# PSUM copies of a token diffusion on VectorE, and a shifted norm two slots earlier in a local attention

## The chip, the cores and the metric

One core of one Trainium2 chip runs the whole program. The metric is the device time of one execution in microseconds (us); lower is better. All data are float32.

The engines of the core have a queue each and run side by side: TensorE (PE; its weight loads, PEld, are listed apart), VectorE (DVE), ScalarE (ACT), GpSimd (POOL) and SyncE (SP), which here issues DMAs. Matrix products land in PSUM, and another engine copies them from there to SBUF. A buffer of PSUM can be filled again only when its reader is done.

## What is computed

Four layers run one after the other on x, 8 sequences of 512 tokens of width 256. Each is `x = x + norm(layer(norm(x)))`: a differential attention, a local attention with a gated feed-forward (two layers deep), a token and channel diffusion, and a mixture of experts. The change touches the second and the third. Cut to what matters:

```python
# local attention and gated feed-forward, twice
h = shift_token(x)                       # half of the features come from the token before
q, k, v = split(h @ wqkv, 3)             # 8 heads of 64
q, k = rotary_xpos(l2norm(q) * qs, l2norm(k) * ksc)
x = x + local_attention(q, k, v) @ wo    # windows of 128, one window back
h = shift_token(x)
h = (h - h.mean()) / sqrt(h.var() + 1e-5) * lg + lb      # the "shifted norm"
a, g = split(h @ w1 + b1, 2)
x = x + (a * gelu(g)) @ w2 + b2

# token diffusion, 16 heads of 16
qk, v = x @ Wqk, x @ Wv
logits = (2 * qk @ qk.T - q2[:, None] - q2[None, :]) / sqrt(dh) * tau
out = softmax(logits) @ v @ Wo
# channel diffusion: the same over channels, 8 groups of 32 channels, on the next norm
```

## The kernel before

The program is written with a tile framework that assigns buffers, inserts the waits, and orders each engine's instructions by their place in the program, unless a priority says otherwise. `high_priority(offset=HOLD)`, with HOLD = 1000, moves an instruction ahead of up to that many others in its engine's order where its inputs allow. Stages are written as generators: work that fills the holes of other work yields, and a `Between` object takes the next part at each call.

**Copies.** `copy` (L156) brings a PSUM tile to SBUF. It takes ScalarE (L160) and VectorE (L162) in turn. `turned` transposes four blocks of 128 tokens into one PSUM bank and copies it; `project` makes a product of two token blocks and hands it to a function that reads it. `moments` (L184 statistics, L186 aggregation, and a step for the reciprocal deviation `rs`) and `normed` (L194) together make a norm over the rows of a tile.

**The local stage** (about 1330 to 2660 us). There are 16 passes c, one for each of two layers and eight sequences. In a pass, eight slots u = 0 to 7 each make the scores of a pair of heads and half the tokens (`scores`: product L642, mask addition L645, maximum, exponential, normalisation on GpSimd), then transpose and copy the weights of the slot before (`turned`, tile lpT), and after every second slot multiply them with the values (`attend`, tile lpo, copied to loT). All PSUM tiles of this stage come from one ring of four tiles of two banks.

In the holes of these slots run two generators. `rotated(c + 1)`, called r, makes queries, keys and values of the next pass: for each of four token blocks a product lqk, a sum of squares, the rotation on VectorE (L607) and GpSimd (L608, L609), and later the transposes (L616) and copies into lqT and lkT. `gated(c - 1)`, called g, finishes the pass before: the output projection is added to y, its rows are shifted by one token into `hs` (DMAs L715 and L716, a copy on GpSimd L717), the shifted norm is made (L720), `hs` is transposed into ghT (L564, L569), and then come the products with w1 (tile lpa), the gate and the products with w2. The table `slots` says how many steps of r and g each slot takes, in order. Half of a slot's calls (rounded up) come before its `turned`, half behind it.

**The diffusion** (about 2676 to 3290 us, and its last sequence's tail to about 3393 us). `tokens` runs over 32 groups of four heads, four token blocks each: `scores` fills two PSUM tiles tsa (L1084) and ScalarE takes their exponentials (L1088); `sums` multiplies these with the values into tpo (L1097) and copies tpo to toc (L1103); `divide` transposes toc and divides. For each sequence `queries` and `squares` make tkT and tqT (L1024, L1025, tq2, L1039), `values` makes tv (L985), and `finish` does what follows a sequence: it transposes to toT, projects with Wo (product pp<-dwo,toT), adds to y, makes the next norm and the channel diffusion (tiles cqk, wc, wvc) and adds the result to x (L950). `finish` and the gate of the experts, with its tiles xf and xT, run as generators between the scores of the next sequence. The tiles pt, pp, tpo and so on come from a ring of two single banks of PSUM; tsa comes from another ring of three tiles of two banks. The last sequence's `finish` runs alone, in the tail.

The program holds two forms of `tokens`, for positive and for other values of tau; with the inputs drawn here, tau is positive and the first form (`known`) is executed.

Of the kernel before, what the change touches and what calls it, by code (L numbers as in the profile page):

```python
# [39 lines left out]
HOLD = 1000  # L40
# [62 lines left out]
class Between:  # L103


    def __init__(self):
        self.work = []
# [13 lines left out]
class Net:  # L121
    def __init__(self, tc, a, out):
        self.tc, self.nc, self.a, self.out = tc, tc.nc, a, out
        self.flip = 0
        self.logs = False


    def begin(self, ctx):
# [26 lines left out]

    def copy(self, out, in_):  # L156

        self.flip ^= 1
        if self.flip:
            self.nc.scalar.copy(out, in_)  # L160
        else:
            self.nc.vector.tensor_copy(out, in_)  # L162
# [374 lines left out]
    def local(self, nb, early, first):  # L537
# [3 lines left out]
        with ExitStack() as ctx:  # L541
# [4 lines left out]
            nc, tc = self.nc, self.tc  # L546
# [227 lines left out]
            first, second = Between(), Between()  # L774
            r, g = first, second
# [10 lines left out]
            r.add(rotated(0))  # L786
            r.end()

            slots = ((g, r), (g, r), (g,), (r, r, r), (r, r, g), (r, r, g), (g, r), (g, r))
            for c in range(total + 1):  # L790
                if c + 1 < total:
                    r.add(rotated(c + 1))
# [74 lines left out]
    def diffusion(self, nb, rest):  # L867

        nc, g = self.nc, self.dw
        later = lambda n, b, **k: rest.enter_context(self.tc.tile_pool(name=n, bufs=b, side="right", **k))
        wk, small, ps = later("t_wk", 1), later("t_small", 3), later("t_ps", 2, space=PSUM)
        tiles = lambda x: [x[:, t, :] for t in range(NT)]
        last = (self.hand[0], wk.tile([P, NT, TH, 16], F32, name="tol", tag="tol"))

        def finish(b, y, o):

            yield
            yield  # L880
            oT = wk.tile([P, DC, S], F32, name="toT", tag="chT")
            self.turned(ps, o.rearrange("p t h e -> p t (h e)"), oT)
            yield

            def add(t0, pp):
                nc.vector.tensor_add(y[:, t0:t0 + 2, :], y[:, t0:t0 + 2, :], pp)

            for t0 in range(0, NT, 2):
                self.project(ps, lambda t: [oT[:, c, self.tok(t)] for c in range(DC)], [g["o"][:, c, :] for c in range(DC)], add, [t0])
                yield  # L890

            made = self.moments(small, tiles(y))
            yield
            h = wk.tile([P, NT, D], F32, name="th", tag="th")
            self.normed(tiles(y), tiles(h), *made)
            yield
            hT = wk.tile([P, DC, S], F32, name="chT", tag="chT")
            self.turned(ps, h, hT, g["g2"], g["b2"])
            yield
            qk = wk.tile([P, NT, D], F32, name="cqk", tag="cqk", bufs=1)  # L900
            for t0 in range(0, NT, 2):
                self.project(ps, lambda t: [hT[:, c, self.tok(t)] for c in range(DC)], [g["cqk"][:, c, :] for c in range(DC)],
                             lambda t0, pp: self.copy(qk[:, t0:t0 + 2, :], pp), [t0])
                yield
            pd = ps.tile([P, DC, P], F32, name="cpd", tag="ps")
            for i in range(DC):
                self.mm(pd[:, i, :], [(qk[:, t, self.tok(i)], qk[:, t, self.tok(i)]) for t in range(NT)])
            dot = small.tile([P, DC, P], F32, name="dot", tag="dot", bufs=1)
            nc.vector.tensor_copy(dot, pd)
            dg = small.tile([P, DC, P], F32, name="dg", tag="dg", bufs=1)  # L910
            nc.vector.tensor_mul(dg, dot, self.ident.unsqueeze(1).to_broadcast([P, DC, P]))
            yield
            pr = ps.tile([P, DC, P], F32, name="cpr", tag="ps")
            self.mm(pr, [(self.const[:, C_ONE:C_ONE + P], dg)])

            nc.vector.scalar_tensor_tensor(dot, dot, 2.0, pr, ALU.mult, ALU.subtract)
            for i in range(DC):
                nc.vector.scalar_tensor_tensor(dot[:, i, :], dot[:, i, :], g["ct"][:, i:i + 1],
                                               self.const[:, C_BLK:C_BLK + P], ALU.mult, ALU.add)
            nm = small.tile([P, DC], F32, name="cnm", tag="cnm")  # L920
            nc.vector.tensor_reduce(nm, dot, AX.X, ALU.max, negate=True)
            rs = small.tile([P, DC], F32, name="crs", tag="crs")
            for i in range(DC):
                nc.scalar.activation(dot[:, i, :], dot[:, i, :], AF.Exp, bias=nm[:, i:i + 1], accum_out=rs[:, i:i + 1])
            nc.vector.reciprocal(rs, rs)
            nc.vector.tensor_mul(dot, dot, rs.unsqueeze(2).to_broadcast([P, DC, P]))
            yield
            yield

            pw = ps.tile([P, DC, D], F32, name="cpw", tag="ps")  # L930
            for i in range(DC):
                self.mm(pw[:, i, :], [(dot[:, i, :], g["co"][:, i, :])])
            wc = wk.tile([P, DC, D], F32, name="wc", tag="wc", bufs=1)
            self.copy(wc, pw)
            yield
            pv = ps.tile([P, DC, D], F32, name="cpv", tag="ps")
            for i in range(DC):
                self.mm(pv[:, i, :], [(g["cv"][:, c, self.tok(i)], wc[:, c, :]) for c in range(DC)])
            wv = wk.tile([P, DC, D], F32, name="wvc", tag="wc", bufs=1)
            self.copy(wv, pv)  # L940
            yield
            yield
            for t0 in range(0, NT, 2):
                if t0:
                    yield
                self.project(ps, lambda t: [hT[:, c, self.tok(t)] for c in range(DC)], [wv[:, c, :] for c in range(DC)], add, [t0])
            made = self.moments(small, tiles(y))
            yield
            self.normed(tiles(y), tiles(y), *made)
            nc.gpsimd.tensor_add(self.xb(b), self.xb(b), y)  # L950
            yield
            self.between.add(self.gate(b, wk, small, ps))

        self.logs = True
        flag = nc.values_load(self.flag, min_val=0, max_val=1)
        with self.tc.If(flag > 0) as known:
            self.tokens(nb, True, wk, small, ps, finish, last)
        with known.Else():
            self.tokens(nb, False, wk, small, ps, finish, last)
        self.joint()  # L960
        self.between = Between()
        self.between.add(finish(nb - 1, *last))
# [5 lines left out]
    def tokens(self, nb, known, wk, small, ps, finish, last):  # L968
# [5 lines left out]
        with ExitStack() as ctx:  # L974
            pool = lambda n, b, **k: ctx.enter_context(self.tc.tile_pool(name=n, bufs=b, **k))
            step, big = pool("t_step", 2), pool("t_big", 3, space=PSUM)
            nc, g = self.nc, self.dw
            state, qk, es, pos, outs = {}, {}, {}, {}, {}
# [3 lines left out]
            def values(b, first=range(0, NT, 2)):  # L982
                hT = state[b][1]
                self.project(ps, lambda t: [hT[:, c, self.tok(t)] for c in range(DC)], [g["v"][:, c, :] for c in range(DC)],
                             lambda t0, pp: nc.scalar.copy(self.tv[b % 2][:, t0:t0 + 2, :, 0:16],  # L985
                                                           pp.rearrange("p t (h e) -> p t h e", e=16)), first)

            def prepare(b):
                y = last[0] if b == nb - 1 else wk.tile([P, NT, D], F32, name="ty", tag="ty", bufs=3)
# [51 lines left out]
            def heads(n):  # L1041

                b, r = divmod(n, 4)
                h = 8 * (r // 2) + r % 2
                return b, slice(h, h + 7, 2)
# [44 lines left out]
            def sums(n, k):  # L1090
                b, h = heads(n)
                if k == 0:
                    pos[n] = ps.tile([P, S], F32, name="tpo", tag="ps")
                e = es.pop((n, k))
                for i in range(4):
                    with self.tc.high_priority(offset=HOLD if i and known else 0):
                        m = nc.tensor.matmul(pos[n][group(i), :], lhsT=self.tv[b % 2][:, k, h.start + 2 * i, :], rhs=e[:, i, :],  # L1097
                                             start=k == 0, stop=k == NT - 1)
                        if i and known:
                            self.tc.keep_in_program_order(m)  # L1100
                if k == NT - 1:
                    oc = step.tile([P, S], F32, name="toc", tag="toc")
                    nc.scalar.copy(oc, pos.pop(n))  # L1103
                    outs[n] = oc

            def divide(n):
# [22 lines left out]
            for s in range(4 * (total + 1) if known else 0):  # L1129
                n, k = divmod(s, 4)  # L1130
# [17 lines left out]
                if k == 1 and n % 4 == 0 and n < total:  # L1148
                    if n // 4 + 1 < nb:
                        ahead.add(prepare(n // 4 + 1))  # L1150
                    if n:
                        b = n // 4 - 1
# [6 lines left out]
            for s in range(0 if known else 8 * (total + 2)):  # L1159
                n, j = divmod(s, 8)  # L1160
# [10 lines left out]
                if j == 5 and 0 <= n - 2 < total:  # L1171
                    divide(n - 2)
                    b = (n - 2) // 4
# [181 lines left out]
    def experts(self, nb, rest):  # L1355


        self.between.end()
        self.logs = False
        rest.close()  # L1360
        with ExitStack() as ctx:
            tiles = ctx.enter_context(ExitStack())
# [3 lines left out]
            nc, tc, g = self.nc, self.tc, self.ew  # L1366
# [191 lines left out]
```

## Time and profile before

| What | us |
|---|---|
| three runs: lowest, median, highest | 3804.09, 3808.49, 3828.85 |
| the profiled execution | 3837.43 |
| its span, from the first instruction to the last | 3835.7 |

The mean TensorE clock that was granted in it is 0.953 of full speed. Times in the profile are counted from the start of the span. In a row of the timeline stand the start, the duration, the engine, the line of the kernel, the operation, its tiles (out<-in), and in brackets the engine's idle time before it and what ended it.

Rows of single groups, that the change moves (mean ns of one, then idle time before it):

```
L985 ACT COPY tv<-pp 128x512 f32<-128x512 f32 x16 | 9.3, 578 | 4.5 <-PE pp L213 4.5
L1103 ACT COPY toc<-tpo 128x512 f32<-128x512 f32 x32 | 18.5, 580 | 14.8 <-issue 9.0 <-PE tpo L1097 5.8
L194 DVE TENSOR_SCALAR hs<-hs,mv,rs 128x256 f32<-128x256 f32 x64 | 37.9, 652 | 1.2 <-ACT rs L170 1.2
```

### The profile page before, as it was taken

The numbers are of one execution on the slowest core, as the hardware profiler recorded it, in microseconds if no ns is written. First come the engines' busy times: TensorE is split into PE (matmuls) and PEld (weight loads), VectorE is DVE, ScalarE is ACT, GpSimd is POOL, SyncE is SP. The second block draws the span as 40 slices with busy tenths as digits, with TensorE's granted clock in tenths as the row PEclk, the third lists the DMA queues.
The fourth block names the chain that finished last, engine by engine and source line by source line (L and its number), as shares of the span: only waits on it lengthen the run. The fifth ranks groups of instructions, "written<-read, shape, count | busy, mean of one in ns | idle before, by whom it ended". The sixth has DMA issues, their size and how long they took to land. (4 is left out here: it accounts for less than half of the span.)

```text
span 3835.7 us, 53567 instructions
## 1 busy us (share of the span) xinstructions
PE 3484.9 (91%) x20034; PEld 1894.1 (49%) x20034; DVE 2201.1 (57%) x4364; ACT 1855.1 (48%) x3719; POOL 1583.6 (41%) x1432
## 2 busy tenths in 40 slices
PE   8999999999987999999999999997988889679985
PEld 3344444444434566665665555564444444446554
DVE  6777777677646666665555666663244443344445
ACT  3555555555543444444444444443655555223334
POOL 3666766676654433333333343321012211153334
PEclk8999999999979999999999999998999999789997
DMA  9300000000001000000010000000000000421115
GB/s 350 119 1 7 6 7 1 7 7 1 6 6 34 3 4 4 4 4 25 4 34 9 9 9 9 9 20 23 1 23 23 23 17 17 147 68 55 53 43 167
DMA packets 95138, 130.29 MB, mean 34 GB/s; under 512 B 24702, under 2 KB 73242, under 8 KB 94874
## 3 DMA queue, kind: packets, MB, share of 16 engines
q1 hardware_dynamic: 88346, 108.94, 8.8%
q0 software_dynamic: 6528, 17.87, 1.3%
q8 instruction: 162, 2.65, 0.3%
q14 instruction: 102, 0.84, 0.1%
HBM read 57.40 MB, written 65.18 MB: 32 GB/s over the span
## 5 line engine op out<-in xcount | busy, mean ns | idle before, releaser
L372 ACT ACTIVATE e<-sa 128x1024 f32<-128x1024 f32 (+3 forms) x512 | 359.4, 702 | 303.7 <-PE sa L365 299.3
L393 POOL TENSOR_TENSOR e<-e,e 128x1536 f32<-128x1536 f32 (+2 forms) x192 | 451.7, 2353 | 91.4 <-PE po L388 81.4
L365 PE MATMUL sa<-qT,kT 32*128 32x512 f32 (+3 forms) x2048 | 431.9, 498 | 9.2 <-ACT e L372 8.8
L369 DVE TENSOR_REDUCE spread<-sc 128x2 f32<-128x256 f32 (+3 forms) x512 | 422.2, 825 | 15.3
L355 PE MATMUL sc<-kT,qT 32*128 32x128 f32 (+3 forms) x2048 | 421.6, 493 | 7.9 <-DVE spread L369 4.5
L656 ACT ACTIVATE lp<-lp,lnm 128x256 f32<-128x256 f32 (+1 forms) x512 | 240.1, 470 | 260.4 <-DVE lnm L648 156.0
L660 POOL TENSOR_TENSOR lp<-lp,lrs 128x1024 f32<-128x1024 f32 x64 | 121.1, 1893 | 529.0 <-DVE lrs L657 508.9
L368 DVE TENSOR_TENSOR sc<-sc,const 128x256 f32<-128x256 f32 x512 | 218.6, 427 | 173.7 <-PE sa L365 140.7
L1088 ACT ACTIVATE te<-tsa 128x1024 f32<-128x1024 f32 x256 | 248.9, 1023 | 135.8 <-PE tsa L1084 88.7
L355 PEld LDWEIGHTS sc<-kT,qT 32*128 32x128 f32 x2048 | 160.7, 189 | 284.9 <-DVE spread L369 113.1
L213 PE MATMUL lpa<-ghT,lw 128*128 128x512 f32 x640 | 284.8, 600 | 12.1 <-ACT ghT L569 12.1
L213 PE MATMUL lqk<-qkv,lhT 128*128 128x512 f32 x512 | 247.7, 622 | 2.3 <-DVE qk L607 1.6
L608 POOL TENSOR_TENSOR qk<-qk,over 128x1024 f32<-128x1024 f32 x64 | 151.4, 2366 | 207.8 <-DVE qk L607 207.8
L375 POOL TENSOR_SCALAR_AFFINE_SELECT e<-e 128x512 f32<-128x512 f32 x256 | 160.5, 640 | 177.0 <-ACT e L372 176.6
L1407 ACT ACTIVATE ehT<-eht,enorm 128x128 f32<-128x128 f32 x288 | 108.3, 457 | 208.6 <-PE eht L1403 207.7
L213 PEld LDWEIGHTS lpa<-ghT,lw 128*128 128x128 f32 x640 | 119.3, 190 | 163.3 <-issue 136.3
L388 PE MATMUL po<-e,v 128*32 128x512 f32 (+3 forms) x2048 | 188.3, 451 | 4.0 <-POOL e L375 3.6
L365 PEld LDWEIGHTS sa<-qT,kT 32*128 32x128 f32 x2048 | 160.9, 190 | 56.4 <-ACT e L372 29.7
L645 DVE TENSOR_TENSOR lp<-lsc,const 128x768 f32<-128x768 f32 (+1 forms) x128 | 138.6, 1083 | 86.5 <-PE lsc L642 85.9
L642 PE MATMUL lsc<-lkT,lqT 64*128 64x256 f32 (+1 forms) x1024 | 156.9, 386 | 28.1 <-DVE qk L607 28.0
L1084 PE MATMUL tsa<-tqT,tkT 32*128 32x512 f32 x1024 | 170.2, 673 | 5.9 <-DVE tqT L1039 3.3
L213 PE MATMUL py<-ew,ehT 128*128 x576 | 145.3, 397 | 23.5 <-ACT ehT L1407 23.5
(294 smaller groups left out, 6811.7 us busy)
## 6 DMA issues: line engine op xcount, KB each, us to landing
xrows<-zero SPq DMA_DIRECT2D x66, 514.0 KB
ex<-xrows SPq DMA_DIRECT2D x72, 128.5 KB
ew<-in_L_ffn_w_dram SPq DMA_DIRECT2D x16, 512.0 KB
egot<-yrows SPq DMA_DIRECT2D x16, 512.0 KB
x<-in_L_attn_X_dram SPq DMA_DIRECT2D x8, 512.0 KB
saved<-x SPq DMA_DIRECT2D x8, 512.0 KB
lx<-saved SPq DMA_DIRECT2D x8, 512.0 KB
xf<-xf SPq DMA_DIRECT2D x8, 512.0 KB
```

What stands on the lines that cost most here:

```text
L213: self.nc.tensor.matmul(out, lhsT=l, rhs=r, start=i == 0, stop=i == len(pairs) - 1)
L355: nc.tensor.matmul(sc[:, i, :w], lhsT=qT[g, self.tok(t)], rhs=kT[g, :w], start=True, stop=True)
L365: nc.tensor.matmul(sa[:, i, :S - k * P], lhsT=kT[g, self.tok(k)], rhs=qT[g, k * P:], start=True, stop=True)
L368: nc.vector.tensor_add(sc[:, :, w - P:w], sc[:, :, w - P:w], own)
L369: nc.vector.tensor_reduce(self.spread[n % 2][:, t, g0:g0 + 2, 0 if n % 2 else 16], sc[:, :, :w], AX.X, ALU.max, negate=True)
L372: nc.scalar.activation(x[:, h0:h0 + 2, :], sa[:, :, :S - k * P], AF.Exp, scale=0.25)
L375: nc.gpsimd.affine_select(x[:, :, :P], x[:, :, :P], [[0, 4], [1, P]], ALU.is_ge, 0.0, base=0, channel_multiplier=-1)
L388: nc.tensor.matmul(pos[n][group(g), k * P:], lhsT=seqs[b][1][:, k, 4 * r + g, :], rhs=x[:, g, :], start=k == 0, stop=k == 2)
L393: nc.gpsimd.tensor_add(y, y, es.pop((n, k)))
L656: nc.scalar.activation(x, x, AF.Exp, bias=nm[:, i, k:k + 1], accum_out=rs[:, i, k:k + 1])
L1084: m = nc.tensor.matmul(sa[i // 2][:, i % 2, :], lhsT=kT[q, self.tok(k)], rhs=qT[q, :], start=True, stop=True)
L1088: nc.scalar.activation(e[:, 2 * i:2 * i + 2, :], sa[i], AF.Exp)
```

## The change

Three edits:

1. A switch `held` is on from the start of the diffusion until the experts. While it is on, every `copy` is one on VectorE with high priority, and the turn between the two engines is not taken.
2. The copies of tv and toc, so far always on ScalarE, go through `copy`. The two additions of products to y in `finish` get the high priority.
3. In the local stage, slots 3, 4 and 5 change from `(r, r, r), (r, r, g), (r, r, g)` to `(r, g, r, r), (r, r), (r, r, g)`. The shifted norm, the second step of g, is so written in slot 3, after the first step of r and before the weights' `turned`, instead of in slot 4 at its end. The number of steps of each generator stays; as half of a slot's calls are made before `turned`, some steps of r also change sides.

```diff
@@ -155,6 +156,11 @@
     def copy(self, out, in_):
 
+        if self.held:
+
+            with self.tc.high_priority(offset=HOLD):
+                self.nc.vector.tensor_copy(out, in_)
+            return
         self.flip ^= 1
         if self.flip:
             self.nc.scalar.copy(out, in_)
@@ -786,7 +792,7 @@
-            slots = ((g, r), (g, r), (g,), (r, r, r), (r, r, g), (r, r, g), (g, r), (g, r))
+            slots = ((g, r), (g, r), (g,), (r, g, r, r), (r, r), (r, r, g), (g, r), (g, r))
@@ -883,7 +889,8 @@
             def add(t0, pp):
-                nc.vector.tensor_add(y[:, t0:t0 + 2, :], y[:, t0:t0 + 2, :], pp)
+                with self.tc.high_priority(offset=HOLD):
+                    nc.vector.tensor_add(y[:, t0:t0 + 2, :], y[:, t0:t0 + 2, :], pp)
@@ -952,6 +959,7 @@
         self.logs = True
+        self.held = True
         flag = nc.values_load(self.flag, min_val=0, max_val=1)
@@ -982,8 +990,8 @@
-                             lambda t0, pp: nc.scalar.copy(self.tv[b % 2][:, t0:t0 + 2, :, 0:16],
-                                                           pp.rearrange("p t (h e) -> p t h e", e=16)), first)
+                             lambda t0, pp: self.copy(self.tv[b % 2][:, t0:t0 + 2, :, 0:16],
+                                                      pp.rearrange("p t (h e) -> p t h e", e=16)), first)
@@ -1100,7 +1108,7 @@
-                    nc.scalar.copy(oc, pos.pop(n))
+                    self.copy(oc, pos.pop(n))
@@ -1357,6 +1365,7 @@
         self.logs = False
+        self.held = False
```

## What the change does to the time, predicted before it ran

> **What bounds the kernel now.** First the page, for the balance of the engines; then the busy time by windows, for the two stages that the change touches.
>
> ```profile
> PE 3484.9 (91%) x20034; PEld 1894.1 (49%) x20034; DVE 2201.1 (57%) x4364; ACT 1855.1 (48%) x3719; POOL 1583.6 (41%) x1432
> ...
> core 0: us, PE busy (x) PEld busy (x) DVE busy (x) ACT busy (x) POOL busy (x), PEclk, DMA share, GB/s
> 1330.00:2550.00 1220.00, 1175.73 (x6274) 737.05 (x6273) 747.49 (x1198) 566.35 (x1431) 436.99 (x316) 0.99 0.04 11
> 2676.00:3290.00 614.00, 549.19 (x3260) 271.32 (x3260) 246.78 (x764) 360.54 (x509) 98.46 (x111) 0.95 0.05 17
> 3290.00:3393.00 103.00, 52.88 (x186) 33.22 (x185) 33.30 (x111) 10.61 (x24) 39.53 (x55) 0.68 0.50 154
> ```
>
> The windows are the local stage, the diffusion loop and the last sequence's tail. TensorE is busy for 1175.73 of 1220 us, 549.19 of 614 and 52.88 of 103, so time can only come out of its idle 44 us, 65 us and 50 us. VectorE has room everywhere (40% busy in the loop), ScalarE too. A copy is therefore worth what TensorE waits for it, not its own duration. So I read the timeline for TensorE's waits. Local stage, one (layer, sequence) pass of 90.8 us (columns: start, duration, engine, line, operation; in brackets the idle time before it and what ended it):
>
> ```profile
> 1841.26 2.35 POOL L608 TENSOR_TENSOR qk<-qk,over 128x1024 f32<-128x1024 f32 x1 [2.39 <-DVE qk L607]
> 1843.69 1.90 POOL L609 TENSOR_TENSOR qk<-qk,ss 128x1024 f32<-128x1024 f32 x1
> 1845.64 1.09 PE L616 MATMUL lpt<-const,qk 128*128 128x128 f32 x8 [0.71 <-POOL qk L609]
> 1850.26 1.13 PE L642 MATMUL lsc<-lkT,lqT 64*128 64x256 f32 x8 [1.85 <-DVE qk L607]
> 1853.15 2.56 DVE L194 TENSOR_SCALAR hs<-hs,mv,rs 128x256 f32<-128x256 f32 x4
> 1862.80 1.44 ACT L569 ACTIVATE ghT<-lpt,lb,lg 128x512 f32<-128x512 f32 x2
> 1863.62 10.57 PE L213 MATMUL lpa<-ghT,lw 128*128 128x512 f32 x24 [1.50 <-ACT ghT L569]
> ```
>
> The shifted norm (`hs`) runs at 1853.15; its transposes, ghT and then the gated product (lpa) come out of it, and lpa waits 1.50 us for ghT. Other waits here are for the rotated heads (POOL L609) and for a ring buffer that DVE L607 frees. Diffusion loop:
>
> ```profile
> 2896.11 0.58 ACT L160 COPY toT<-pt 128x512 f32<-128x512 f32 x1 [0.42 <-PE tsa L1084]
> 2896.19 0.69 DVE L162 COPY toT<-pt 128x512 f32<-128x512 f32 x1 [5.04 <-PE tsa L1084]
> 2896.74 3.57 PE L213 MATMUL pp<-dwo,toT 128*128 128x256 f32 x8 [1.26 <-ACT toT L160]
> ...
> 2946.79 2.37 POOL L950 TENSOR_TENSOR x<-x,ty 128x1024 f32<-128x1024 f32 x1 [1.19 <-DVE ty L194]
> 2949.19 1.41 DVE L184 BATCH_NORM_STATS2 st<-x 128x6 f32<-128x256 f32 x4 [2.49 <-POOL x L950]
> 2951.35 0.57 ACT L985 COPY tv<-pp 128x512 f32<-128x512 f32 x1
> 2951.97 1.13 PE L213 MATMUL tq<-tsq,const 128*128 128x512 f32 x2 [2.30 <-ACT tv L985]
> 2956.40 0.66 PE L205 MATMUL pt<-const,xf 128*128 128x128 f32 x4 [0.96 <-DVE tqT L1039]
> ```
>
> One toT copy starts late on ScalarE (its queue is full of exponentials), and the product behind it waits 1.26 us; tq waits 2.30 us for the ring buffer that tv's copy frees.
>
> **The change part by part.** The sum is made against the profiled execution, 3837.43 us (span 3835.7), which lies 0.76% above the median of the three runs, 3808.49; I carry the difference over to the median.
>
> *The copies.* In the branch that runs, 80 copies go from ScalarE to VectorE: tv 16 at 578 ns (row tv<-pp), toc 32 at 580 ns, and one each per sequence of toT, cqk, wc and xT, 32 at about 585. ScalarE loses 46.6 us, VectorE gains 80 x 0.69 (row DVE toT) = 55 us, about 302 of 614 us busy. That raises no bound; what counts is order. From the two kernels' instruction orders, per sequence:
> - toT: both halves now stand on VectorE directly behind their transposes, where it was idle for 5.04 us. The waits of pp<-dwo,toT sum to 10.1 us over the six full sequences; two VectorE copies end to end leave about 0.3 us of each. Gain 1.3 to 1.7; I take 1.5.
> - tv: its first copy now stands on VectorE behind four statistics of x, which wait for POOL's addition L950 (ends 2949.16), three more, and a normalise. VectorE executes in order, so it can't pass them. By their rows it ends near 2952.85 rather than at 2951.92: tq's wait grows from 2.30 to about 3.2. Loss 0.9.
> - toc: 0.11 us dearer, but no longer behind an exponential of 1.02 us, so it ends 0.6 earlier. The tqT chain, for which pt<-xf waits (0.96 us), comes behind tv and toc and ends at 2956.95 instead of 2956.34. That 0.6 and the dearer copy make a loss of 0.7 for tv and toc together.
> - cqk, wc, xT and the additions to y with high priority: their consumers stand at least one run of exponentials (4 us) behind in TensorE's order, and that run hides them. Without that cover each would cost at most its 0.11 us difference. If VectorE were late, they would cost its backlog, up to the 2.5 us wait above.
>
> Net −1.5 + 0.7 = −0.8 us x 6 = −5 us. In the tail TensorE and VectorE take turns, so a copy on the dearer engine counts in full: about 4 x 0.11 to 0.15 = +0.5 us. The moves add no DMA there.
>
> *The shifted norm, fourth slot instead of the end of the fifth.* Per pass, the 4 statistics, 4 aggregations, ScalarE's two steps for rs, 4 normalisations and later 8 transposes and ghT all stay; only place changes. The four DMAs that shift the rows are issued 1828.88 to 1831.26 and land about 3 us later; the statistics now stand at 1836.8, so near 2.5 us of slack is left, and SP's queue has nothing behind them that is needed sooner. Replaying the slots by hand with the rows above: three statistics ahead of the sums of squares delay the heads' chain by 0.29 us (L609 ends 1845.87 for 1845.59). rs is ready at 1842.75. Then the four normalisations. Alone they cost 4 x 0.40 = 1.6 us, but here they meet two POOL operations back to back. The profile has that neighbour too:
>
> ```profile
> 1318.47 2.76 DVE L194 TENSOR_SCALAR x<-x,mv,rs 128x256 f32<-128x256 f32 x2
> 1318.63 2.45 POOL L608 TENSOR_TENSOR qk<-qk,over 128x1024 f32<-128x1024 f32 x1 [0.56 <-DVE qk L607]
> 1321.16 1.90 POOL L609 TENSOR_TENSOR qk<-qk,ss 128x1024 f32<-128x1024 f32 x1
> 1322.02 1.19 DVE L194 TENSOR_SCALAR x<-x,mv,rs 128x256 f32<-128x256 f32 x1
> ```
>
> A normalisation that starts beside L608 ends with it, and a later one ends with L609. **A rule speaks against the change here.** The Trainium skill, page "SBUF — State Buffer", on the port pair that VectorE and GpSimd share, calls it an exclusive lock: whoever starts first holds it for the whole instruction, and the other is fully blocked. hs where it runs now meets one lock (2.56 us for 1.6). By the rule the new place can meet two, so the norm ends at about 1846.7, as in the rows above; by hs's own row it ends at 1845.3, and unblocked at 1844.4. What waits behind it on VectorE is the mask addition (L645) of the next scores, its maximum, and the copy lpT, which attention needs. With the double lock lpT is ready at 1849.8, the last heads end at 1855.6, and the gated product starts at 1862.8 instead of 1863.62: −0.8 us a pass. With one lock −1.8, with none −2.1. I take −0.8, the nearest row for the neighbour. 14 steady passes: −11 us. The bounds are −29 us, and, if VectorE runs later than I replay, a loss (below).
>
> Sum: −11 − 5 + 0.5 = −16 us: the profiled execution 3821, the median 3792.
>
> **The rivals.**
> *Faster (0.16).* The normalisation misses the locks (−2 x 14 = −28), and the diffusion's ring waits shrink as the edit says, tv included because the statistics' wait on L950 also shortens: six times the waits for toT 1.5, tv 1.5, tqT 0.7 = −22. About −50: 3758. For: 65 us of idle TensorE in that window. Against: tv's place in VectorE's order.
>
> *Hidden (0.14).* Nothing in the local stage moves, because lpa's start is set by the attention chain (lpo, loT) and not by ghT. Only diffusion's −5 to +5 is left: 3803 to 3813. For: ghT's wait is only 1.50 us, and half of it can return as the next wait.
>
> *Slower (0.20).* VectorE's order in the fourth slot. Normalisations held by both locks stand in front of the mask addition L645, which frees the lsc buffer and feeds the exponentials. In the replay the break-even is an end of the norm near 1847.5, only 0.8 us behind the one that I take. Past it every us goes through lpT, lpo, loT and the last heads. If the norm instead makes POOL wait (the lock works both ways), L609 ends late and the transposes at 1845.64, which wait for it already, slip in full. At 1.5 us lost a pass, +21; with tv's 0.9 x 6 = +5, about +26: 3835. With both, up to 3 us a pass, it passes 3850. For: waits at 1845.64 and 1850.26 show that the heads' chain is critical in just these slots. Against: VectorE is only 61% busy.
>
> That the change doesn't do what it says is out: the order shows all 80 copies and the moved norm.
>
> **How the numbers follow.** The forecast, −5 to −35 us, has 0.50; its own range is 3774 to 3804. The range leaves out the far halves of the faster and the slower case: 3764 to 3835. One per cent, 38 us (below 3770 or above 3847), is about what a measurement can tell from no change. Faster by that takes most of the faster case: 0.13. Slower takes the part of the slow case with 3 us a pass: 0.10. Within it: 0.77.
>
> **What would show it.** In the changed profile the pass's period falls from 90.8 to about 90.0; hs's normalisations last about 3.9 us where they overlap L608 and L609; lpa's wait for ghT shrinks and lqk's heads end later than lpa's other inputs. tq's wait is led by VectorE's tv and is near 3.2 us; the waits for toT are below 0.5 us. I am wrong if the period grows, if the transposes' wait at L616 grows, or if TensorE's idle time in the loop stays near 65 us with new names.

## The result, and the profile after

The changed kernel takes 3823.51 us (median of 13 runs, 3812.63 to 3828.62), the kernel before 3810.6 us (13 runs, 3804.09 to 3828.85): a ratio of 1.0028, 95% interval 1.0015 to 1.0041. It is slower by 0.28%, about 11 us, where 16 us less was forecast. Yet the profiled execution of the changed kernel has a span of 3811.9 us, 24 less than the 3835.7 of the profile that the prediction was made from. So the first thing to settle is which two profiles can be compared.

The changed kernel's page has this line of busy times:

```profile
PE 3478.5 (91%) x20034; PEld 1898.6 (50%) x20034; DVE 2287.4 (60%) x4444; ACT 1811.1 (48%) x3639; POOL 1582.8 (42%) x1432
```

The 80 copies have moved: ScalarE is 44 us down and VectorE 86 us up, about 52 of it behind the local stage and 31 in it, where the moved norms last longer. TensorE's work is the same 20034 instructions. Busy time by window, cut where the stages begin: the local stage from the first projected sum, the diffusion loop from its first tsa to its last, then tail and experts. The changed kernel:

```profile
core 0: us, PE busy (x) PEld busy (x) DVE busy (x) ACT busy (x) POOL busy (x), PEclk, DMA share, GB/s
1277.20:2658.30 1381.10, 1318.12 (x6955) 825.48 (x6953) 867.78 (x1383) 631.31 (x1583) 482.81 (x359) 0.98 0.04 12
2658.30:3259.90 601.60, 550.40 (x3254) 271.67 (x3256) 293.22 (x829) 318.34 (x433) 97.06 (x109) 0.94 0.05 17
3259.90:3811.90 552.00, 416.56 (x1660) 280.91 (x1652) 259.29 (x699) 185.49 (x506) 207.30 (x287) 0.89 0.29 92
```

The kernel before, in the later profile before_again (span 3804.7 us), cut the same way:

```profile
1273.60:2666.80 1393.20, 1318.94 (x6959) 822.67 (x6957) 837.15 (x1383) 633.74 (x1584) 483.40 (x359) 0.98 0.04 12
2666.80:3255.60 588.80, 541.43 (x3256) 269.15 (x3256) 244.65 (x754) 357.23 (x507) 97.19 (x109) 0.95 0.05 18
3255.60:3804.70 549.10, 416.07 (x1660) 278.63 (x1652) 256.13 (x694) 188.44 (x511) 207.43 (x287) 0.89 0.29 92
```

The local stage is 12.1 us shorter, about as forecast. The loop is 12.8 us longer, and tail with experts 2.9 us longer. The last figure is not clear of scatter: the first stage, which the change does not touch, differs by 3.6 us. In the profile of the prediction the same loop of the same kernel had lasted 609.8 us: against that one the changed loop looks 8 us faster, against this one 13 slower. What decides here is therefore the ratio of runs on one chip, and profiles from one chip.

The local stage of the changed kernel, timeline of one pass (start, duration, engine, line, operation; idle time before it and what ended it):

```profile
1832.34 2.35 POOL L614 TENSOR_TENSOR qk<-qk,over 128x1024 f32<-128x1024 f32 x1 [2.57 <-DVE qk L613]
1833.48 3.98 DVE L200 TENSOR_SCALAR hs<-hs,mv,rs 128x256 f32<-128x256 f32 x4
1834.77 1.90 POOL L615 TENSOR_TENSOR qk<-qk,ss 128x1024 f32<-128x1024 f32 x1
...
1839.29 1.22 DVE L168 COPY lpT<-lpt 128x1024 f32<-128x1024 f32 x1
1840.56 1.09 PE L696 MATMUL lpo<-lpT,lv 128*64 128x128 f32 x16 [1.30 <-DVE lpT L168]
...
1853.14 5.42 PE L219 MATMUL lpa<-ghT,lw 128*128 128x512 f32 x12 [0.45 <-ACT ghT L575]
```

The shifted norm takes 3.98 us where it took 2.56: it is held by both POOL operations, one after the other (its first normalisation ends at 1834.84, 0.15 us behind L614's end). TensorE's wait for ghT is down from 1.50 to 0.45 us, and a wait of 1.30 us for the copy lpT, which stands behind the norm on VectorE, is new.

The diffusion loop of the changed kernel, the place where tq waits:

```profile
3011.23 2.37 POOL L957 TENSOR_TENSOR x<-x,ty 128x1024 f32<-128x1024 f32 x1 [1.19 <-DVE ty L200]
3013.63 1.40 DVE L190 BATCH_NORM_STATS2 st<-x 128x6 f32<-128x256 f32 x4 [2.48 <-POOL x L957]
...
3016.50 0.68 DVE L162 COPY tv<-pp 128x512 f32<-128x512 f32 x1
3017.24 1.13 PE L219 MATMUL tq<-tsq,const 128*128 128x512 f32 x2 [3.13 <-DVE tv L162]
```

From the start of the statistics to tq it is 3.61 us; in before_again it is 2.78 (3011.07 to 3013.85). TensorE waits 3.13 us before tq where it waited 2.29 there.

### The profile page after: what moved, and what is told of

Read it like the earlier page. It is cut to its first block, busy times and chain, and to the rows that moved or that the text cites. A ratio compares the mean times of both kernels' runs of the same rounds, so it can differ in the third digit from the quotient of the medians.

```text
span 3811.9 us, 53546 instructions
## 1 busy us (share of the span) xinstructions
PE 3478.5 (91%) x20034; PEld 1898.6 (50%) x20034; DVE 2287.4 (60%) x4444; ACT 1811.1 (48%) x3639; POOL 1582.8 (42%) x1432
## 5 line engine op out<-in xcount | busy, mean ns | idle before, releaser
L614 POOL TENSOR_TENSOR qk<-qk,over 128x1024 f32<-128x1024 f32 x64 | 151.0, 2360 | 173.2 <-DVE qk L613 171.4
L670 POOL TENSOR_TENSOR lp<-lp,lrs 128x256 f32<-128x256 f32 (+1 forms) x128 | 103.0, 825 | 220.2 <-DVE lrs L663 220.2
```

## The experiments

They ran on five chips, here called A to E. The medians of the kernel before were 3810.8, 3815.6, 3841.0, 3838.7 and 3840.2 us, so only ratios within a chip are compared. The ratios below are to the kernel before on the same chip, with their 95% intervals.

### Chip A: which of the two parts loses

Theory A: the moved norm gains and the copies lose more. Theory B: the moved norm loses in the runs that were not profiled.

slots_only, the kernel before with

```diff
-            slots = ((g, r), (g, r), (g,), (r, r, r), (r, r, g), (r, r, g), (g, r), (g, r))
+            slots = ((g, r), (g, r), (g,), (r, g, r, r), (r, r), (r, r, g), (g, r), (g, r))
```

> Only the slot table of the local stage is changed. Theory A (the moved norm shortens each pass from 90.8 to about 89.2 us as the profile of the changed kernel shows, and the loss comes from elsewhere): the local stage (first product behind the first pass to the first tsa) is about 12 us shorter and the whole about 3798 us, ratio 0.997. Theory B (the moved norm is the loss, in the runs that were not profiled): ratio at or above 1.003.

copies_only, the changed kernel with that line turned back:

> All edits of the diffusion, the old slot table. Theory A (the copies cost more than the moved norm gains, by waits on VectorE or by a lower TensorE clock in the diffusion loop): about 3810 + 13 + 12 = 3835 us, ratio near 1.006, and a granted clock below that of the kernel before. Theory B: ratio at or below 0.999.

Each kernel once more, for a second profile, after_again and before_again:

> The changed kernel once more, for a second profile. If the clock decides, an execution of about 3824 us shows a longer diffusion loop than the 601.6 us of the first profile (3813.6 us), with more time at half clock there, and a local stage that is unchanged (1381 us from the first projected sum to the first tsa).

> The kernel before once more, for a second profile and its granted clocks run by run. If the clock decides, its runs lie near 3810 us at a mean clock near 0.955, above the 0.949 that the changed kernel's runs show in the middle, and its diffusion loop lasts about 600 us in a usual run, less than the 609.8 of the profile of before (3837.4 us).

Measured: slots_only 3800.16 us, ratio 0.9968 (0.9955 to 0.9982); copies_only 3836.25 us, 1.0062 (1.0047 to 1.0078); after_again 3818.71 us, 1.0022 (1.0013 to 1.0031); before_again 3810.83 us, 1.0004 (0.9992 to 1.0016). Theory A holds, and the parts add up: 0.9968 x 1.0062 = 1.0030. The moved norm is worth 10.7 us, the copies cost 25 us. The second profile of the changed kernel repeats the first (loop 601.8 us), that of the kernel before doesn't (588.8 for 609.8). slots_only is faster than both kernels.

Where the local stage's gain comes from is read in the waits of TensorE (who waits for whom: us in total, times, longest). Before_again:

```profile
PE lsc L642 <- DVE qk L607: 24.0, 13, 1.9
PE lpa L213 <- ACT ghT L569: 12.1, 13, 1.5
PE lpt L616 <- POOL qk L609: 9.3, 13, 0.7
```

slots_only:

```profile
PE lpo L690 <- DVE lpT L162: 20.4, 15, 1.8
PE lpo L690 <- DVE lp L645: 7.4, 13, 0.6
PE lpa L213 <- ACT ghT L569: 4.1, 9, 0.5
PE lsc L642 <- ACT lv L624: 3.1, 7, 0.5
```

45.4 us of waits are down to 35.0 in these rows. The norm that left the later slot frees the ring buffer and the heads' chain there, and it delays lpT where it went.

### Chip B: is it tv's place on VectorE?

Theory T: tv's copy stands behind statistics that wait for POOL, and this wait, made longer, is the loss. Rivals: the loss is spread over the other copies; or what matters is not the wait but TensorE's clock.

tv_on_act, copies_only with tv back:

```diff
-                             lambda t0, pp: self.copy(self.tv[b % 2][:, t0:t0 + 2, :, 0:16],
+                             lambda t0, pp: nc.scalar.copy(self.tv[b % 2][:, t0:t0 + 2, :, 0:16],
```

> The edits of the diffusion with the old slot table, but tv's copies stay on ScalarE. Theory T (tv's place on VectorE behind the statistics of x makes the wait, and the longer wait trips the half clock): the wait of tq falls back from 3.2 to 2.3 us a sequence, the time at half clock in the loop from 87 to about 57 us, and the time from 3836 to about 3811 us, ratio 1.000. Rival S (the loss is spread over toc, toT, cqk and the additions to y on a fuller VectorE): ratio stays above 1.004.

tv_alone, the kernel before with nothing but tv's copy on VectorE with high priority:

> The kernel before with only the copies of tv moved to VectorE with high priority. Theory T: most of the loss, ratio about 1.005, tq waits 3.2 us, half clock near 80 us in the loop. Rival S: ratio below 1.002.

fill, copies_only with added products ahead of tq (cut; `self.zero` is a tile of zeros):

```diff
+                for j in range(5 if known and k == NT - 1 and n % 4 == 2 else 0):
+                    for i in range(4):
+                        with self.tc.high_priority(offset=HOLD):
+                            m = nc.tensor.matmul(pos[n][group(i), :], lhsT=self.zero, rhs=e[:, i, :], start=False, stop=False)
```

> The edits of the diffusion with the old slot table, and in the gap ahead of the waiting tq 20 more matmuls a sequence (zeros times the exponentials, added to tpo, so the result is the same; about 2.4 us of TensorE work that lies inside the 3.2 us wait). Theory C (the half clock that the gap brings is the larger part of the loss, not the gap): the half clock around tq goes, 20 to 40 us of it in the loop, and the time falls by 8 to 20 us, from 3836 to 3816 to 3828, though TensorE does more work. Rival W (only the wait itself counts): 3836 or slower, by up to 14 us if the added work isn't hidden.

tvf3_slots, the changed kernel with the gate's statistics behind tv (cut; `self.head` is tv's last copy):

```diff
+        yield
+        yield
+        yield
+        with ExitStack() as order:
+            if self.head is not None:
+                order.enter_context(tc.issue_after(self.head))
+            made = self.moments(small, tiles(self.xb(b)))
-        made = self.moments(small, tiles(self.xb(b)))
```

> The whole change, and the statistics of x for the experts' gate are put behind tv's copy in the order (three steps later in the generator, and ordered behind the copy), so that no copy stands on VectorE behind the wait for GpSimd. Theory T: tq's wait falls to under 1 us a sequence, time at half clock in the loop to 40 us or less, the loop to about 575 us and the time to about 3785 us, ratio 0.993. Rival (the later gate is waited for in turn by xT, the gate's product or the ring behind it): ratio 0.997 or above, the gain of the slot table alone.

Measured: tv_on_act 1.0043 (1.0028 to 1.0058), tv_alone 1.0005 (0.9996 to 1.0014), fill 1.0116 (1.0094 to 1.0137), tvf3_slots 1.0147 (1.0127 to 1.0166). Theory T falls on this chip by tv_alone: tq waits 18.8 us in all instead of 13.8, the loop still lasts 589.0 us (588.8 in before_again on chip A), and the time is the same. A wait of TensorE that grows isn't yet time lost.

tv_on_act says less than it seems to. With tv back on ScalarE tq was expected to wait 2.3 us again; it still waits 3.14. Before_again, then tv_on_act:

```profile
3009.63 1.92 PE L1097 MATMUL tpo<-te,tv 128*32 128x512 f32 x16
3013.85 2.08 PE L213 MATMUL tq<-tsq,const 128*128 128x512 f32 x2 [2.29 <-ACT tv L985]
...
3023.74 1.13 PE L219 MATMUL tq<-tsq,const 128*128 128x512 f32 x2 [3.14 <-ACT tv L993]
3024.80 1.07 PE L1105 MATMUL tpo<-te,tv 128*32 128x512 f32 x8
```

tv's copy is as early as before, 2.77 us from the statistics to tq. But 8 of the 16 tpo products now stand behind tq, so TensorE comes to tq earlier and waits longer for it. Moving toc with high priority makes this: toc_alone has the same order of TensorE's instructions as tv_on_act, while pairs_alone and no_priority (below) have that of the kernel before. Nor is the half clock around tq the loss here: in tv_on_act the loop has 56.3 us at half clock, as before_again has 56.7, and 0.43% is still lost.

fill decides nothing on the clock, since it didn't do what it was meant to. Its timeline:

```profile
2965.54 4.47 PE L1108 MATMUL tpo<-te,zero 128*32 128x512 f32 x40
...
2975.57 0.95 PE L213 MATMUL pt<-const,xf 128*128 128x128 f32 x4 [2.43 <-DVE toc L164]
```

The added products took 4.47 us, not 2.4; they delayed toc, and the gap came back one step later, with the half clock behind it (89.5 us of it in the loop, 87.1 in that of copies_only).

In tvf3_slots the waits of TensorE are these:

```profile
PE tpt L1129 <- DVE toc L162: 11.4, 4, 4.2
PE pt L211 <- DVE th L200: 6.8, 4, 1.9
PE pt L211 <- DVE toc L162: 5.7, 2, 5.4
PE tsa L1099 <- ACT te L1103: 5.6, 9, 2.7
```

tq's wait is gone from the list, and waits for toc and the exponentials have taken its place; the loop is 627 us. The gate also ends later, which lengthens the tail: tail and experts take 575.9 us.

### Chip C: the other copies, and the priority

pairs_alone keeps only the switch in `copy` (toT, cqk, wc, wvc, xT), on the kernel before (cut):

```diff
+        if self.held:
+
+            with self.tc.high_priority(offset=HOLD):
+                self.nc.vector.tensor_copy(out, in_)
+            return
```

> The kernel before with only the copies of toT, cqk, wc, wvc and xT held on VectorE with high priority; tv and toc stay on ScalarE, the additions to y as before. Theory D (two halves that two engines copied side by side now stand one behind the other on VectorE, 0.7 us a pair, which counts in full where TensorE and VectorE take turns): the tail up to the experts' first transposes about 2.8 us longer (110.4 for 107.6), the loop 4 to 10 us longer, ratio 1.002 to 1.004. Rival E (the loss belongs to toc, whose 32 copies reorder TensorE's products): ratio at or below 1.001.

toc_alone changes only toc (`moved` is a copy on VectorE with high priority, as above; tv_alone uses it for tv):

```diff
-                    nc.scalar.copy(oc, pos.pop(n))
+                    self.moved(oc, pos.pop(n))
```

> The kernel before with only the 32 copies of toc on VectorE with high priority. Theory D: ratio near 1.000 to 1.001, the tail unchanged at about 107.6 us. Rival E: ratio 1.003 or more, by a longer loop.

no_priority is copies_only without any high priority, the additions' too (cut to the copies):

```diff
         if self.held:
 
-            with self.tc.high_priority(offset=HOLD):
-                self.nc.vector.tensor_copy(out, in_)
+            self.nc.vector.tensor_copy(out, in_)
             return
```

> All copies and additions of the diffusion's edits on VectorE, but none with high priority; old slot table. Theory D (the engine, not the priority): about as slow as with priority, ratio 1.005 to 1.007. Rival P (the priority puts short copies ahead of the normalisations on the chain and reorders the products): ratio below 1.003.

Measured: pairs_alone 1.0020 (1.0006 to 1.0033), toc_alone 1.0025 (1.0013 to 1.0036), no_priority 1.0050 (1.0031 to 1.0070). The loss is spread: pairs and toc together give 1.0045, and tv_on_act, which holds both, gave 1.0043 on chip B. Rival P falls: without priority, and with TensorE's order as before, the copies are about as slow as with it. The high priority of the two additions was not run by itself.

### Chips D and E: added waits, or the half clock

The records of TensorE's clock know two states, full and half, and change in steps of 3.41 us. Theory H: the moved copies cost by the time at half clock, not by added waits; then TensorE's busy time grows by half of the added time at half clock. Rival W: added waits.

Chip D had the kernel before and the three parts alone, chip E the kernel before, copies_only and tv_on_act; the edits are those above.

> The kernel before, for a profile on the same chip as the three parts of this call. Its loop and its time at half clock there are what the parts are compared with; by theory H (a part costs by the half clock that its shifted waits bring) the loop's busy time on TensorE differs between the kernels by half of the difference in time at half clock, within 2 us.

> Only toc's copies on VectorE, once more, beside a profile of before on the same chip. Theory H: loop 8 to 12 us longer than before_c's, most of it busy time of TensorE with 10 us or more of added half clock. Rival W (added waits alone): TensorE's idle time in the loop up by 6 us or more and its busy time within 3 us.

> Only the copies of toT, cqk, wc, wvc and xT on VectorE, once more. Theory D (halves one behind the other): tail about 1 to 3 us longer than before_c's; and the loop 4 to 8 us longer. Theory H or rival W for the loop, as for toc.

> Only tv's copies on VectorE, once more: the way from the statistics of x to tq is 0.84 us longer than in before_c as in the first profile of the whole change, the loop within 3 us of before_c's, ratio 1.000 to 1.001.

> The kernel before, for a profile on the chip of this call: the loop near 589 us if this chip is of the first kind (as in the first four experiments), near 620 us if it is of the second.

> All edits of the diffusion, old slot table, on another chip. Theory H: the loop's TensorE busy time grows over before_d's by half of what the time at half clock grows by, within 3 us (14.4 us for 30.5 us in the first pair), and the waits add about 4 us; ratio 1.005 to 1.008. Rival W: busy time within 3 us of before_d's, and idle time up by 10 us or more.

> The same with tv's copies left on ScalarE. If tv's longer way costs by what the clock makes of it, the loop is 3 to 9 us shorter than copies_only_d's; if tv costs nothing here either, within 2 us of it. Ratio 1.004 to 1.006.

Times: before_c 1.0000 (0.9989 to 1.0012), toc_alone_c 1.0026 (1.0010 to 1.0043), pairs_alone_c 1.0032 (1.0020 to 1.0044), tv_alone_c 1.0052 (1.0031 to 1.0072); before_d 1.0003 (0.9989 to 1.0016), copies_only_d 1.0078 (1.0050 to 1.0106), tv_on_act_d 1.0063 (1.0043 to 1.0083). tv alone, which lost nothing on chip B, loses 0.5% on chip D.

The loop in the windows view, copies_only on chip A (to be read against the 588.80 us and 541.43 us busy of before_again):

```profile
2670.70:3277.30 606.60, 555.79 (x3256) 275.43 (x3256) 292.97 (x829) 318.56 (x433) 97.17 (x109) 0.93 0.05 17
```

before_d:

```profile
2674.20:3283.50 609.30, 547.42 (x3254) 270.08 (x3256) 244.70 (x754) 358.63 (x507) 97.34 (x109) 0.95 0.05 17
```

copies_only_d:

```profile
2677.40:3304.90 627.50, 565.46 (x3256) 277.62 (x3256) 293.15 (x829) 319.24 (x433) 97.07 (x109) 0.93 0.05 17
```

| loop, us | length | TensorE busy | idle | at half clock |
|---|---|---|---|---|
| chip A: before_again | 588.8 | 541.4 | 47.4 | 56.7 |
| chip A: after_again | +13.0 | +9.2 | +3.8 | +17.8 |
| chip A: copies_only | +17.8 | +14.4 | +3.4 | +30.5 |
| chip E: before_d | 609.3 | 547.4 | 61.9 | 56.6 |
| chip E: copies_only_d | +18.2 | +18.1 | +0.1 | +37.2 |
| chip E: tv_on_act_d | +17.9 | +18.3 | -0.5 | +30.8 |
| chip D: before_c | 620.2 | 559.1 | 61.1 | 81.5 |
| chip D: toc_alone_c | +6.6 | +2.7 | +3.9 | -4.7 |
| chip D: pairs_alone_c | +2.4 | +0.7 | +1.7 | +2.4 |
| chip D: tv_alone_c | +8.9 | +5.1 | +3.8 | +26.0 |

(The last column is summed from the clock records of the loop.) For the changed kernel and for all copies together the profiles agree with theory H: half of the added half clock is 8.9, 15.2 and 18.6 us, the added busy time 9.2, 14.4 and 18.1, and the added waiting 3.8, 3.4 and 0.1. Without tv on chip E half is 15.4 and the busy time 18.3; that loop is no shorter than with tv. With the busy time at half clock counted half, copies_only has only 0.4 us more work than before_again, and copies_only_d 1.4 more than before_d. Rival W is out there.

For the parts alone single profiles don't settle it, because they scatter: the loop of the kernel before has 56.6 us at half clock in before_d and 81.5 in before_c, as far apart as tv_alone_c and before_c. The granted clock of every run is on record, though, as a mean over its span. A run of span s and mean clock c has 2 x (1 − c) x s at half clock; over the runs of the kernel before this scatters by 13 to 22 us (standard deviation) on each chip. In the runs of the kernel before, chip by chip, a us more at half clock goes with 0.28 to 0.37 us of time (correlation 0.88 to 0.97); over the runs of all these kernels, each around its own mean, it is 0.31. Means of all runs against the kernel before on the same chip, in us:

| kernel, chip (runs) | time | at half clock | 0.31 of that | rest |
|---|---|---|---|---|
| slots_only, A (11) | -10.0 | +16.2 | +5.0 | -15.0 |
| after_again, A (22) | +8.7 | +47.1 | +14.6 | -5.9 |
| copies_only, A (6) | +25.5 | +56.6 | +17.5 | +8.0 |
| copies_only_d, E (4) | +23.4 | +40.5 | +12.5 | +10.9 |
| no_priority, C (9) | +21.2 | +44.1 | +13.7 | +7.5 |
| tv_on_act, B (6) | +15.9 | +17.7 | +5.5 | +10.4 |
| tv_on_act_d, E (5) | +17.3 | +32.5 | +10.1 | +7.2 |
| toc_alone, C (22) | +10.1 | +4.7 | +1.5 | +8.7 |
| toc_alone_c, D (8) | +11.2 | +8.9 | +2.8 | +8.4 |
| pairs_alone, C (22) | +7.5 | +25.5 | +7.9 | -0.4 |
| pairs_alone_c, D (10) | +10.9 | +36.8 | +11.4 | -0.5 |
| tv_alone, B (14) | +1.8 | +7.3 | +2.3 | -0.5 |
| tv_alone_c, D (4) | +15.6 | +43.0 | +13.3 | +2.2 |

(Standard errors are 1 to 3 us for the time and 4 to 11 for the half clock; the split is an estimate: in the TensorE-bound loop the profiles above show nearly the full half, and so the rests beside much half clock may be smaller.) The parts differ in kind. What the pairs and tv lose goes with the half clock, and tv, with the same added wait, loses on chip D where it brings 43 us of half clock and not on chip B where it brings 7. toc loses 7 to 9 us outside the clock, whether 0.31 or the full half is taken, and by the factor 0.31 every kernel with the old slot table that moves toc has a rest of 7 to 11 us, every one that doesn't of about 2 at most. In toc_alone_c's loop TensorE waits 3.9 us more and has 6.7 us more work by the same count as above.

How one wait goes with half clock is seen where tq waits, in windows of 3.41 us that are cut where the clock's own steps lie (length, then PE busy first, PEclk third from the end). before_d:

```profile
2945.81:2949.22 3.41, 1.94 (x17) 0.42 (x16) 1.95 (x10) 0.36 (x2) 1.43 (x1) 1.00 0.00 0
2949.22:2952.64 3.42, 2.20 (x10) 0.61 (x10) 3.42 (x14) 2.10 (x5) 0.00 (x0) 1.00 0.07 24
2952.64:2956.05 3.41, 2.22 (x16) 1.15 (x16) 3.41 (x8) 2.88 (x6) 0.00 (x0) 1.00 0.38 132
2956.05:2959.46 3.41, 3.41 (x32) 2.52 (x28) 1.45 (x6) 2.17 (x3) 0.00 (x0) 1.00 0.02 5
```

copies_only_d, the same place of the loop:

```profile
2958.89:2962.30 3.41, 2.06 (x17) 0.42 (x16) 1.83 (x9) 0.37 (x2) 1.54 (x1) 1.00 0.00 0
2962.30:2965.72 3.42, 1.64 (x10) 0.61 (x10) 3.42 (x10) 1.04 (x3) 0.00 (x0) 1.00 0.00 0
2965.72:2969.13 3.41, 2.56 (x15) 1.24 (x8) 3.41 (x10) 1.68 (x4) 0.00 (x0) 0.50 0.44 154
2969.13:2972.54 3.41, 3.41 (x15) 1.57 (x14) 2.26 (x6) 1.78 (x4) 0.00 (x0) 0.50 0.00 0
2972.54:2975.96 3.42, 3.42 (x17) 3.26 (x17) 0.38 (x2) 1.42 (x3) 0.00 (x0) 0.50 0.02 5
2975.96:2979.37 3.41, 3.41 (x13) 1.55 (x12) 1.48 (x5) 1.12 (x3) 1.36 (x2) 0.50 0.00 0
2979.37:2982.78 3.41, 3.41 (x27) 2.06 (x29) 3.10 (x17) 0.82 (x1) 0.00 (x0) 1.00 0.00 0
```

The first window is nearly the same in both. In the second TensorE is busy for 2.20 us before and 1.64 us after, because tq comes later. At 2.20 of 3.42 the clock stays full; behind 1.64 of 3.42 stand four windows at half clock. Counted on the clock's steps over the loops of the four profiles of all copies and before on chips A and E: of 47 windows at full clock in which TensorE was busy for less than half, 44 were followed by one at half clock; of 579 in which it was busy for half or more, 7 were. So far as these traces go, what counts is the busy share of a window, and where a wait falls in it decides: of the six waits of 2.3 us before tq in before_again, three lie in windows under half busy.

## Why the prediction was wrong

**The shifted norm** was right: forecast -11 us, measured -10.7 us in the time and -12.4 us in the stage's length (1393.2 to 1380.8 in slots_only). The double lock is there: the first two normalisations of 14 passes last 1.37 and 2.06 us, where the first lasted 1.59 and the second 0.40, and all four 3.98 us; 3.9 was forecast. The row of `x` that had both POOL operations beside it, and the rule of the Trainium skill's page "SBUF — State Buffer", section "Who interferes with whom", gave the size; the two POOL operations last 2.35 and 1.90 us as before, so the lock cost VectorE alone. The copy named as standing behind the norm, lpT, is the new wait. In the steady passes the period is 89.2 us in most and up to 90.5 in some, for about 90.8. That the sum fits so closely is partly luck: the gain was -0.8 us a pass by forecast and is -1.1 over the 13 periods between the first and the last steady norm (1180.1 to 1165.6 us), and by the table of runs about 5 us of it go back to the clock.

**The copies** were wrong, and by their sign: -4.5 us forecast, +25 us measured on chip A. Three terms failed: the gain of -9 us (6 x 1.5) that toT was to bring is not there; TensorE's clock, with which most of the loss goes, was put at nothing; and toc, a small gain in the sum, loses 7 to 9 us besides. Step by step:

1. *toT, "gain 1.3 to 1.7; I take 1.5".* The step read the wait behind toT as ScalarE's lateness. The two rows that it showed say otherwise: the copies start at 2896.11 and 2896.19, both are released by TensorE, and VectorE had been idle for 5.04 us. A copy that starts 0.08 us before an idle engine's isn't late for want of its engine. (The waits before this product sum to 8.7 us in that profile, not to 10.1.) With both copies on VectorE the wait stays where it exists (in the view of waits 8.7 + 0.9 us in before_d, 11.1 in copies_only_d), and on chip A it doesn't exist. before_again there:

```profile
2880.05 0.69 DVE L162 COPY toT<-pt 128x512 f32<-128x512 f32 x1 [2.02 <-PE pt L205]
2880.42 0.62 ACT L160 COPY toT<-pt 128x512 f32<-128x512 f32 x1
2881.09 1.99 PE L213 MATMUL pp<-dwo,toT 128*128 128x256 f32 x8
```

copies_only_d:

```profile
2907.73 0.69 DVE L162 COPY toT<-pt 128x512 f32<-128x512 f32 x1 [3.59 <-PE tsa L1092]
2908.48 0.70 PE L219 MATMUL pp<-dwo,toT 128*128 128x256 f32 x2 [1.38 <-DVE toT L162]
```

2. *"Without that cover each would cost at most its 0.11 us difference".* The halves of toT, cqk and xT had run side by side on two engines and now run one behind the other, so that the second can cost a whole 0.69 us copy where nothing covers it. pairs_alone costs 0.20 to 0.32%, with TensorE's order as before and, by the table of runs, all of it with the half clock; that the order of the halves brings this is argued, not shown. In the tail, forecast at +0.5 us, the experts' first transposes (eht) come 2.8 us later in copies_only (110.4 us after the loop, for 107.6) and 1.8 us in the changed kernel, but 0.6 us in pairs_alone_c and 0.9 us earlier in copies_only_d, each against its own chip: so the tail doesn't show it either.

3. *tv and toc, "Loss 0.9" and "a loss of 0.7 for tv and toc together".* The size of tv's delay was right, 0.83 us on the way from the statistics to tq. Its worth was not: nothing on chip B, 0.5% alone on chip D, with the half clock. toc, counted as a small gain within that sum, costs 0.25% alone, most of it outside the clock. With toc alone TensorE's products are ordered anew (in the whole change too, in part differently), for which the prediction had no term; but no_priority, without the new order, has a rest of the same size, so which wait makes toc's loss is open.

4. *The clock was in no term of the sum.* The prediction counted idle time only ("time can only come out of its idle 44 us, 65 us and 50 us"). In the loop of copies_only 14.4 of 17.8 added us, and 18.1 of 18.2 on chip E, are TensorE's own work at half clock, behind windows that fall under half busy. The view by windows, which showed 0.95, would have asked for it. The Trainium skill, page "TensorE: Matmul & The Clock Gate", section "HAM oscillation — how this bites in real kernels", warns of idle gaps over about 3.4 us; here gaps of 1.3 to 3.2 us were enough in 40 of the 44 windows counted above.

And a basis was wrong. The profile of the prediction lay 0.76% above the median, and the prediction carried that over evenly. It lay in single stages: the loop was 609.8 us there and 588.8 in before_again, with the waits for toT among what differs. On chip E the same kernel's loop is 609.3 us, with those waits.

**The slower rival** had the sign, not the place: it put +21 us into the local stage, which became faster, and +5 us on tv.

Left open: why the loop of one kernel differs by 20 to 30 us between chips; what of toc's move costs the 7 to 9 us outside the clock; and what would happen at a held clock, since no run changed the clock alone (fill was to do it and didn't). That the half clock is paid for is shown by TensorE's busy time and by the runs; that the moved copies bring it through single waits is seen at tq and is an inference for the rest.

## What to carry to other kernels

Before a wait is put down to a busy engine, look at when the other engine's twin of the same operation starts and what released it; if both start together, the producer is late. Two halves that go to two engines in turn are a pair in parallel, and to put both on the emptier engine can cost one whole copy wherever it isn't covered. On a TensorE that is 90% busy, cut the loop into the clock's windows before and after: the same 0.8 us of wait cost nothing on one chip and 0.5% on another, by the half clock that it brought. And where the record has a clock for every run, compare the means of all runs, not two profiles. When one edit is run alone, look at the order of the other engines too: the framework may have changed it.

## What the hardware showed that was not expected

The clock of TensorE went to half behind 44 of 47 windows of 3.41 us that were under half busy, in loops that are 90% busy overall, and once stayed there for four windows (13.7 us) although TensorE was fully busy in three of them. The same kernel has a median of 3810.8 us on chip A and 3841.0 on chip C; instructions of one form on the other engines last equally long (a tsa exponential 1.02 us on chips A and E). Between the loops of before_again and before_d, 588.8 and 609.3 us, 14.5 us are TensorE's idle time and 6.0 its busy time, at the same 57 us of half clock.
